# Holding the first five convolution taps of tile 0 behind the softmax's subtraction in even units

## The chip, the cores and the metric

The kernel runs on one core of one Trainium2 chip. The metric is device time in microseconds (us). Before the change the median of three runs is 3747.22 us (3746.66 to 3749.31). A core has five engines with their own instruction streams: TensorE (PE; its weight loads are listed as PEld), VectorE (DVE), ScalarE (ACT), GpSimd (POOL) and SyncE (SP), which issues the large DMAs. [...]

## The reference, cut to what matters

The input x is (8, 384, 64, 64) in f32: eight images of 384 channels. Two layers follow each other, each with a group norm in front and a residual addition behind.

```python
# layer 0: window attention, half of the heads on windows shifted by 4
x = x + attention(_gn(x))      # LayerNorm -> qkv -> two branches -> proj
#   per 8x8 window: softmax(q k^T * SCALE + bias [+ mask]) v
# layer 1: frequency filter on 8x8 blocks, depthwise 3x3 convolution, gate
x = x + ffn(_gn(x))
#   t = w_in . x ; t = irfft2(rfft2(t) * filter) ; t = conv3x3_depthwise(t)
#   x1, x2 = t[:, :192], t[:, 192:] ; out = w_out . (gelu(x1) * x2)
```

All of it is computed in f32, and the output is x after both layers.

## The kernel before

An image is cut into 8 strips of 8 rows (NS = 8); a strip is 384 channels by 512 pixels, held as 128 partitions by 3 tiles of 512. Time is counted in units. Unit u of an image covers one branch of one strip: even units the plain windows (br = 0), odd units the shifted ones (br = 1), so 16 units per image and 128 in all. While the attention of image b runs, the second layer of image b - 1 runs in the same units: a strip of it takes two units per stage, and its stages (mix, transform, back, convolution, gate, finish) follow each other over about six units.

The function calls are collected in a plan: at(place, piece, ...) gives each piece a place in units, and the pieces are called in the order of these places. On TensorE this order is kept, as every matmul and transpose is marked with keep_in_program_order. On the other engines the Tile scheduler orders the instructions: it keeps a simulated clock, and on each engine takes the earliest instruction of the program among those that it holds to be ready. An instruction planned late can so be taken early, in time that the engine would have stood idle. The function behind(i, other, NoSync, ...) adds an edge that keeps i after another instruction in this ordering, without a semaphore.

The pieces that matter here:

- scores (TensorE, PSUM tile pS), weights (VectorE: bias additions L456, maximum L460, subtraction L463, which is stored as zs["soft"]), exponent (ScalarE, L469), turn (TensorE transposes pT), apply (TensorE, pA) and normalise (VectorE: reciprocal L503 and product L504, the weighted values' norm), put (TensorE transposes po; copies L527 to L537). In the plan, weights of a unit stands at 0.12, and normalise of the unit before at 0.07.
- Projection: pr, with L546 adding the residual.
- LayerNorm: ln_sums (matmuls ln, ScalarE's m L347, VectorE's L349, L350 and L352, two DMAs that spread the line), ln_scale (VectorE, L363), shifted_half (GpSimd, L376 to L378).
- qk_tile (matmuls pq; ScalarE copies them to qab, kab, qcd, kcd, L394) and v_tile (pvv; L428).
- Second layer: mix (pt, copied by L584), transform (pf; product with the filter on VectorE, L601), back (pz, copied with borders by ScalarE, L629 to L633, to a tile z).
- conv: for each of the tiles m = 0, 2, 1 of a strip, the centre tap is a scaled copy by ScalarE (L667), and taps 1 to 8 are a chain of eight scalar_tensor_tensor on VectorE (L673), each adding a shifted z to the accumulator zz. Taps 1 to 5 use rows that are there once the strip's own z is; taps 6 to 8 need the first row of the next strip and come two units later. Taps 1 to 5 of tile 0 are planned at 0.68 to 0.92 of an even unit, those of tiles 2 and 1 in the odd unit after it, and taps 6 to 8 of the strip before at 0.20 to 0.45 of the even unit. All of b = B - 1, the last image, is left out of the rules below.
- gate (ScalarE's Gelu L686, L687; VectorE L688 to L690) and finish (matmuls pw; VectorE adds the residual from PSUM, L706; SyncE stores the strip). The maximum L460 of an even unit is held behind the last L706.

PSUM tiles of the pool "gemm" (four buffers) serve pq, pvv, pr, pt, pf, pz, pw and ln in turn; tiles of the pool "att" (two buffers) serve pS, pT, pA and po. TensorE waits for a buffer until it has been read.

The program also pads TensorE's stream with empty instructions. FETCHES counts instructions per piece, WAITS estimates the wait instructions (5.325 per unit), and RUN_AT gives the place within 256 at which a stretch is to begin; small_tiles marks where this is worked out.

Of the kernel before, what the change touches and what calls it, by code (L numbers as in the profile page):

```python
# [38 lines left out]
def block_kernel(ctx: ExitStack, tc: tile.TileContext, out, x, consts, fsel, wqk, wv, bqk, bv,  # L39
                 wp, bp, lng, lnb, rpb1, rpb2, w_in, w_dw, w_out, filt):  # L40
    nc = tc.nc
    B = x.shape[0]
# [35 lines left out]
    def row512(tag, bufs, name):  # L78
        return sb.tile([P, ST], F32, tag=tag, bufs=bufs, name=name)
# [209 lines left out]
    def behind(i, other, kind, reason):  # L289
        tc.add_manual_dep(i.ins, other.ins.name, mybir.DependencyInfo(kind, mybir.DependencyReason.DATA),  # L290
                          reason=reason)
# [366 lines left out]
    def conv(b, s, m, tap):  # L658

        z = zs[b, s, m]  # L660
        n = on_pe[s].get(m, 0) if b == B - 1 else 0
        if tap < max(n, 1):
            return
        if tap == max(n, 1):
            zz = row512("zz", 5, f"zz_{b}_{s}_{m}")
            if n == 0:
                nc.scalar.activation(zz.rearrange("p (r c) -> p r c", c=SW), z[:, 1:9, 1:SW + 1], AF.Copy,  # L667
                                     scale=dw_sb[:, m, 4:5])
                zs[b, s, "zz", m] = zz
            zs[b, s, "acc", m] = zz  # L670
        acc, old = zs[b, s, "acc", m], zs[b, s, "zz", m]
        dy, dx = TAPS[tap] // 3, TAPS[tap] % 3
        i = nc.vector.scalar_tensor_tensor(acc.rearrange("p (r c) -> p r c", c=SW),  # L673
                                           z[:, dy:dy + 8, dx:dx + SW], dw_sb[:, m, TAPS[tap]:TAPS[tap] + 1],
                                           old.rearrange("p (r c) -> p r c", c=SW), ALU.mult, ALU.add)

        if b < B - 1 and m and tap == 1:
            tc.keep_in_program_order(i)
        if b < B - 1 and tap == 6:
            behind(i, zs["soft"], mybir.DependencyClass.NoSync, "softmax first")  # L680
        zs[b, s, "zz", m] = acc

# [30 lines left out]
    for b in range(B):  # L713
# [62 lines left out]
        for s in range(NS):  # L776
            u = first + 2 + 2 * s
            at(u - 0.84, load, b, s, "mix")
            at(u + 0.02, normal_x1, b, s)
            for i in range(4):  # L780
                at(u + (0.28, 0.45, 0.60, 0.78)[i], mix, b, s, i)
            for j in range(2):
                at(u + (0.995, 1.02)[j], transform, b, s, j)
            if b < B - 1:
                at(u + 1.985, small_tiles, u + 2)
            at(u + 1.99, back, b, s)

            for n, m in enumerate((0, 2, 1)):
                for tap in range(1, 6):
                    at(u + (2.62, 3.15, 3.5)[n] + 0.06 * tap, conv, b, s, m, tap)  # L790
                for tap in range(6, 9):
                    at(u + 4.2 + 0.25 * (n * 3 + tap - 6) / 9, conv, b, s, m, tap)
            if b == B - 1:
                at(u + 2.3, conv_taps, b, s)
            at(u + 5.16, load, b, s, "finish")
            at(u + 4.5, gate, b, s)
            at(u + 6.10, finish, b, s)
# [130 lines left out]
```

## Time and profile before

| what | value |
|---|---|
| median of three runs | 3747.22 us |
| profiled execution, its own time | 3747.89 us |
| its span | 3745.9 us |
| TensorE busy, weight loads busy | 3638.7 us (97%), 2315.4 us (62%) |
| VectorE busy | 2838.6 us (76%) |
| ScalarE busy | 2378.3 us (63%) |
| GpSimd busy | 439.2 us (12%) |
| granted TensorE clock | 0.996 |
| L673, the taps on VectorE | 1490 instructions, 1105.9 us, mean 760 ns |

A line of a timeline has start, duration, engine, source line, operation, what it writes and reads, how many instructions were merged, and, in brackets, how long the engine stood idle before it and what ended that. Matmuls come from two helper functions, so nearly all of them carry L62 or L72 and are told apart by their tiles. In a list of waits a row tells who waited for whom, with us in total, times, and the longest in us.

### The profile page before, as it was taken

What the parts mean: (1) busy time and instruction counts of PE and PEld (TensorE: products, weight loads), DVE (VectorE), ACT (ScalarE), POOL (GpSimd) and SP (SyncE); (2) the same over time, 40 slices, a digit from 0 to 9 for tenths busy, and PEclk for the clock granted to TensorE, in tenths of its full rate; (3) what the DMA queues carried; (4) which work ended last, traced back from release to release, by engine and by line L of the source; (5) the groups of instructions that cost most, each with busy time, mean ns of one, the idle gap of its engine ahead of it and who ended that gap; (6) DMA issues with size and microseconds to landing.
All of it is one profiled execution on the core that took longest, in us unless ns stands there. A gap on an engine that the chain in (4) does not pass through costs nothing.

```text
span 3745.9 us, 92754 instructions
## 1 busy us (share of the span) xinstructions
PE 3638.7 (97%) x38144; PEld 2315.4 (62%) x38144; DVE 2838.6 (76%) x4601; ACT 2378.3 (63%) x3946; POOL 439.2 (12%) x776
## 2 busy tenths in 40 slices
PE   4999999999999999999999999999999999999898
PEld 3666666666666666666666666666666666666554
DVE  4554578777887687777887778877788777777898
ACT  1766676666676576665766766666676666676442
POOL 5111011111101011101101011111111111110000
PEclk9999999999999999999999999999999999999999
DMA  4222222323322233323332322323233222222422
GB/s 121 86 83 74 91 100 100 107 90 108 118 103 83 88 133 108 116 80 116 109 113 84 117 95 100 133 80 109 99 113 109 99 88 83 100 80 82 151 102 76
DMA packets 144506, 377.32 MB, mean 101 GB/s; under 512 B 12308, under 2 KB 12900, under 8 KB 144100
## 3 DMA queue, kind: packets, MB, share of 16 engines
q1 hardware_dynamic: 139952, 370.60, 28.3%
q8 instruction: 318, 5.21, 0.6%
q0 software_dynamic: 2048, 0.15, 0.1%
q10 hardware_dynamic: 2100, 0.63, 0.1%
q14 instruction: 88, 0.72, 0.1%
HBM read 270.54 MB, written 100.79 MB: 99 GB/s over the span
## 4 chain that ended last, share of the span: by engine, by line
PE 84%; DVE 6%; ACT 4%; DMA 3%; issue 2%; POOL 0%; SPq 0%; ACTq 0%; DVEq 0%; POOLq 0%
PE pq L62 23%; PE pr L62 13%; PE pt L62 12%; PE pvv L62 12%; PE pw L62 6%; PE pS L62 3%; PE pA L62 3%; PE pz L62 3%; DVE zz L673 3%; PE pT L72 3%; PE po L72 2%; PE pf L62 2%; PE ln L62 2%; PE pc L62 1%; DMA rpb_raw<-in_rpb_dram 1%
## 5 line engine op out<-in xcount | busy, mean ns | idle before, releaser
L673 DVE SCALAR_TENSOR_TENSOR zz<-z,dw_sb,zz 128x512 f32<-128x512 f32 x1490 | 1105.9, 760 | 195.4 <-ACT zz L667 172.7
L62 PE MATMUL pq<-y,wqk_sb 128*128 128x512 f32 x2160 | 990.2, 596 | 0.0
L62 PEld LDWEIGHTS pq<-y,wqk_sb 128*128 128x128 f32 x2160 | 402.7, 190 | 456.2 <-issue 424.2
L62 PE MATMUL pt<-wi_sb,xn 128*128 128x384 f32 x1536 | 535.2, 487 | 8.1 <-DVE x_finish L706 8.1
L62 PE MATMUL pr<-oT,wp_sb 128*128 128x512 f32 x1152 | 523.1, 592 | 1.0 <-DVE oT L537 1.0
L62 PE MATMUL pvv<-wv_sb,y 128*128 128x192 f32 x2880 | 496.5, 326 | 2.5 <-ACT kcd L394 2.5
L62 PEld LDWEIGHTS pvv<-wv_sb,y 128*128 128x128 f32 x2880 | 471.6, 190 | 40.1 <-issue 21.3
L394 ACT ACTIVATE qab<-pq,bq_sb,cst 96x512 f32<-96x512 f32 (+1 forms) x256 | 198.0, 773 | 402.9 <-PE pq L62 386.0
L62 PEld LDWEIGHTS pt<-wi_sb,xn 128*128 128x128 f32 x1536 | 286.0, 190 | 213.9 <-issue 49.0
L394 ACT ACTIVATE kcd<-pq,vec 32x512 f32<-32x512 f32 x512 | 348.9, 681 | 9.0
L62 PEld LDWEIGHTS pr<-oT,wp_sb 128*128 128x128 f32 x1152 | 211.1, 190 | 224.4 <-issue 209.7
L376 POOL COPY y<-y 128x384 f32<-128x384 f32 x112 | 100.2, 894 | 1583.1 <-PE pvv L62 1089.3
L349 DVE TENSOR_TENSOR lr<-m 128x128 f32<-128x128 f32 x64 | 19.7, 308 | 301.9 <-ACT m L347 301.8
L335 POOL TENSOR_TENSOR sq<-sq 128x512 f32<-128x512 f32 x128 | 167.8, 1311 | 637.2 <-ACT sq L333 632.2
L667 ACT ACTIVATE zz<-z,dw_sb 128x512 f32<-128x512 f32 x183 | 133.8, 733 | 166.1 <-PE pw L62 160.5
L394 ACT ACTIVATE qcd<-pq,bq_sb,cst 96x512 f32<-96x512 f32 (+1 forms) x256 | 197.3, 771 | 43.8 <-PE pq L62 40.4
L546 DVE SCALAR_TENSOR_TENSOR x_add<-pr,vec,x_add 128x512 f32<-128x512 f32 x192 | 143.4, 747 | 103.3 <-PE pr L62 101.5
L584 ACT COPY t<-pt 128x384 f32<-128x384 f32 x256 | 125.0, 488 | 141.6 <-PE pt L62 138.7
L428 ACT COPY v<-pvv 128x384 f32<-128x384 f32 x256 | 121.8, 481 | 129.7 <-PE pvv L62 129.3
L62 PE MATMUL pw<-zz,wo_sb 128*128 128x512 f32 x384 | 181.9, 610 | 0.0
L394 ACT ACTIVATE kab<-pq,vec 96x512 f32<-96x512 f32 (+1 forms) x256 | 174.4, 681 | 9.1 <-PE pq L62 7.4
L469 ACT ACTIVATE e<-e 128x1024 f32<-128x1024 f32 x128 | 135.3, 1057 | 68.2 <-DVE e L463 66.8
(139 smaller groups left out, 5272.6 us busy)
## 6 DMA issues: line engine op xcount, KB each, us to landing
x_add<-in_x_dram SPq DMA_DIRECT2D x64, 768.0 KB
x1d<-x_add SPq DMA_DIRECT2D x64, 768.0 KB
x_mix<-x1d SPq DMA_DIRECT2D x64, 768.0 KB
x_finish<-x1d SPq DMA_DIRECT2D x64, 768.0 KB
out_dram<-x_finish SPq DMA_DIRECT2D x64, 768.0 KB
x_norm<-in_x_dram SPq DMA_DIRECT2D x61, 768.0 KB
x_stats<-in_x_dram SPq DMA_DIRECT2D x56, 768.0 KB
rs<-line SPq DMA_DIRECT2D x62, 256.0 KB
```

The costliest lines, as they stand in the source:

```text
L62: tc.keep_in_program_order(nc.tensor.matmul(*args, **kw))
L72: tc.keep_in_program_order(nc.tensor.transpose(*args, **kw))
L335: nc.gpsimd.tensor_tensor(sq[:, 0, :], sq[:, 0, :], sq[:, k, :], ALU.add)
L349: nc.vector.tensor_tensor(rc, m[:, 0:P], m[:, 0:P], ALU.mult)
L376: nc.gpsimd.tensor_copy(dst[:, :, :, :, 0:4], src[:, :, :, :, 4:8])
L394: return nc.scalar.activation(dst[to:to + n], pq[of:of + n], AF.Identity, bias=bias[of:of + n], scale=scale)
L428: nc.scalar.copy(v[:, 2 * g:2 * g + 2, :, 0:HD], pvv[:, 0:384].rearrange("p (g h d) -> p g h d", g=2, h=4))
L469: nc.scalar.activation(e, e, AF.Exp)
L546: nc.vector.scalar_tensor_tensor(t[:, m, :], pr, bp_sb[:, m:m + 1], t[:, m, :], ALU.add, ALU.add)
L584: nc.scalar.copy(t1, pt[:, 0:C])
L667: nc.scalar.activation(zz.rearrange("p (r c) -> p r c", c=SW), z[:, 1:9, 1:SW + 1], AF.Copy, scale=dw_sb[:, m, 4:5])
L673: i = nc.vector.scalar_tensor_tensor(acc.rearrange("p (r c) -> p r c", c=SW), z[:, dy:dy + 8, dx:dx + SW], dw_sb[:, m, TAPS[tap]:TAPS[tap] ...
```

## The change

One condition is widened. Tap 6 of each tile was held behind the latest softmax subtraction already; now tap 1 of tile 0 is too, in all images but the last. As taps 2 to 5 add to the accumulator of tap 1, they follow it. At the place of this call in the plan the latest subtraction is that of the same even unit.

```diff
         if b < B - 1 and m and tap == 1:
             tc.keep_in_program_order(i)
-        if b < B - 1 and tap == 6:
+        if b < B - 1 and (tap == 6 or m == 0 and tap == 1):
             behind(i, zs["soft"], mybir.DependencyClass.NoSync, "softmax first")
         zs[b, s, "zz", m] = acc
```

## The prediction

> **What bounds the kernel now.** I read the page's busy times first, then the list of what TensorE waited for, then the timelines of two even units. The profiled execution took 3747.89 us with a span of 3745.9; 2.0 us lie around the span. The median of the runs is 3747.22, 0.7 below the profiled one.
>
> ```profile
> PE 3638.7 (97%) x38144; PEld 2315.4 (62%) x38144; DVE 2838.6 (76%) x4601; ACT 2378.3 (63%) x3946; POOL 439.2 (12%) x776
> ...
> q8 instruction: 318, 5.21, 0.6%
> ...
> PE 84%; DVE 6%; ACT 4%; DMA 3%; issue 2%; POOL 0%; SPq 0%; ACTq 0%; DVEq 0%; POOLq 0%
> ```
>
> TensorE (PE) is the bound, and its program order is fixed. Its busy time may hide pitch, so I also took the distance between successive matmul starts: from 600 to 3500 us it shows the same few stalls as the waits below and no others. VectorE (DVE, 76%) can only matter where TensorE waits for it, directly or through ScalarE (ACT). From the answer on TensorE's waits (us in total, times, longest):
>
> ```profile
> PE pT L72 <- ACT e L469: 9.0, 8, 1.4
> PE pz L62 <- DVE t L601: 8.9, 15, 3.0
> PE pt L62 <- DVE x_finish L706: 8.1, 6, 1.4
> PE pz L62 <- ACT v L428: 7.3, 13, 1.0
> ...
> PE pvv L62 <- ACT kcd L394: 2.5, 6, 0.6
> ```
>
> The third line is the one that VectorE's order in even units makes; the last is made through ScalarE. The first line's waits are nearly all in odd units, the second's in the last image, which the change leaves out. Now VectorE and TensorE around 1838 us, an even unit with the first strip of an image:
>
> ```profile
> 1828.70 0.26 DVE L503 RECIPROCAL rc<-pA 128x16 f32<-128x16 f32 x1
> 1828.99 0.96 DVE L504 TENSOR_TENSOR o<-pA,rc 128x768 f32<-128x768 f32 x1
> 1831.91 2.43 DVE L673 SCALAR_TENSOR_TENSOR zz<-z,dw_sb,zz 128x512 f32<-128x512 f32 x2 [1.96 <-ACT zz L667]
> 1834.26 0.68 DVE L456 TENSOR_TENSOR e<-pS,bias 128x512 f32<-128x512 f32 x1
> ...
> 1835.46 2.31 DVE L673 SCALAR_TENSOR_TENSOR zz<-z,dw_sb,zz 128x512 f32<-128x512 f32 x3
> 1837.69 1.88 DVE L706 TENSOR_TENSOR x_finish<-pw,x_finish 128x512 f32<-128x512 f32 x3
> ...
> 1840.72 1.22 DVE L463 TENSOR_TENSOR e<-e,mx 128x1024 f32<-128x1024 f32 x1
> ...
> 1838.42 2.20 PE L62 MATMUL pt<-wi_sb,xn 128*128 128x384 f32 x6 [1.35 <-DVE x_finish L706]
> ```
>
> Two and three taps (L673), five in all, stand ahead of the residual additions (L706) that empty the PSUM tiles pw; pt (the fence's last line, from TensorE's own timeline) needs a tile of the same pool and starts late. These five are taps 1 to 5 of tile 0. In the common even unit around 1210 us they begin even before the norm (L503, L504):
>
> ```profile
> 1210.26 1.54 DVE L673 SCALAR_TENSOR_TENSOR zz<-z,dw_sb,zz 128x512 f32<-128x512 f32 x2 [3.86 <-ACT zz L667]
> 1211.71 0.25 DVE L503 RECIPROCAL rc<-pA 128x16 f32<-128x16 f32 x1
> ...
> 1215.89 1.88 DVE L706 TENSOR_TENSOR x_finish<-pw,x_finish 128x512 f32<-128x512 f32 x3
> ...
> 1218.92 1.23 DVE L463 TENSOR_TENSOR e<-e,mx 128x1024 f32<-128x1024 f32 x1
> ```
>
> Here pt starts at 1218.73, 2.1 us after the first addition ended: no stall.
>
> **What the Trainium skill says.** "Perfetto Trace Analysis", Identifying the Most-Contended Engine: matmul busy time is a poor measure of distance to the limit, since matmuls overlap; I used start distances for that reason, and they agree with the waits. "SBUF — State Buffer", SBUF: two separate sides: a VectorE instruction with two SBUF inputs and a GpSimd one exclude each other on a shared port for a whole instruction. The trace agrees: the tap at 1832.70 took 1.64 us, against 0.74 usually, while GpSimd's addition of squares ran from 1830.83 to 1833.79. "Perfetto Trace Analysis", Identifying Dependency Chains: an instruction that waits for several engines may get EventSemaphore instructions ahead of it; TensorE shows 687. "Runtime: NRT & Kernel Launch", Instruction fetch mechanics: instructions are fetched in blocks of 256, mostly hidden; the 318 fetches of q8 are TensorE's 81,516 records divided by 256. The last two make my slower rival.
>
> **The change part by part.** It adds one ordering edge per tile 0, on one engine: no instruction, no DMA and, both ends being VectorE's, no semaphore wait. It concerns 54 even units (7 images by 8 strips, less two units after the last softmax). Five taps move behind the softmax's subtraction (L463). In front of them the nine last taps of the strip before are already held there and come earlier in the plan, so the five will mostly fill VectorE's gaps later in the unit.
>
> *First strips, six units with a stall* (942, 1390, 1838, 2286, 2735, 3184 us). By the rows above: the norm ends at 1829.95; the two bias additions take 1.27 (1834.26 to 1835.53) and end near 1831.2, pS being done at 1828.8; pw's last six matmuls start at 1830.78 with 0.43 us each, so the three tiles are ready near 1831.8, 1832.7 and 1833.5, and the first addition ends near 1832.5. The transposes po start at 1836.04, eight by 0.109 us, so pt can start at 1836.91 and has 4.4 us to spare. In these six units pt starts 1.62 us after the last po, in the other fifty 0.11: saved 6 x 1.51 = 9.1 us. (The waits row's 8.1 leaves out part of the pitch.)
>
> *Last strips of six images, and the very first unit*: matmuls pvv wait for ScalarE's kcd copies in six of them, the start distance after pT being 0.59, 0.61, 0.63, 0.68, 0.70 and 0.90 against 0.11 us: 3.5 us. Around 1780 the subtraction ends at 1791.27 with four taps in front of it, 4 x 0.73 = 2.9 us plus waits for the shared port. Without them: norm to 1780.6, statistics (1.87) to 1782.4, biases to 1783.5, additions to 1785.4, maximum and subtraction (1.20 + 1.21) to 1787.8. ScalarE's exponent, at 1791.30, is then held only by ScalarE itself, whose table load ended at 1789.47: 1.8 us earlier, and kcd was 0.5 to 0.8 us late. I take all 3.5; the bounds are 0 and 3.5.
>
> *The other 42 units*: no wait of TensorE here goes back to these taps. The exponent ends 5.2 us or more before its transposes in every even unit of the steady part. 0 us. What hides the moved 5 x 0.70 = 3.5 us (a row of five takes 3.51) is VectorE's idle time before the LayerNorm's first step (L349), 2.9 to 7.6 us in these units, plus about 1.1 us ahead of the gate. Around 1210: the norm no longer stands behind taps that wait for ScalarE and can start 1.5 us earlier, at 1210.2, but pw holds the additions until about 1216, so the subtraction gains about 1.6 of the 3.5 us and 1.9 are left to absorb, 0.8 after the gate's gap. That fits even 2.9. If that cover were gone, each us late at L349 passes through the LayerNorm's line DMAs to the odd unit's scaling (L363), subtraction and exponent; there the cover is 2.7 to 4.3 us, but only 0.05 to 0.4 us in one or two odd units per image.
>
> *Queues.* SyncE's store of the finished strip waits for the last addition, so it and the loads queued behind it leave 1.6 to about 3.4 us earlier; nothing waits longer. GpSimd's 2.6 to 3.0 us of squares run early in the first-strip units, where the taps leave; in the common unit GpSimd is almost idle until 1236.
>
> *Sum*: 9.1 + 3.5 = 12.6 against the profiled 3747.9, that is 3735.3; 3734.6 against the median. I predict 3735, whose own range is 3730 to 3740.
>
> **Rivals.** *No change that counts* (3740 to 3754). The planner places instructions by its own estimates. If it fills the place before the additions with other ready work (statistics, normalisation), or if a new wait of about 1 us per image appears on ScalarE, the 12.6 shrinks below 7.5. For it: nine of the 12 us sit in six units only. Against it: in those units VectorE stood idle for 1.96 us ahead of the taps, so nothing else was ready.
>
> *Slower through the instruction blocks* (3755 to 3785). The planner pads TensorE's stream so that block boundaries miss the stretch of tiny matmuls, with a fixed estimate of 5.325 wait instructions per unit. Counting TensorE's records, that stretch begins at place 241 of a block around 570 us and at 233 to 235 near the end. In the two early units where the place was 209 or 210, matmuls there started about 0.8 us late. If the new order takes away one wait instruction per two units, the place drifts some 50 by the end; it becomes slower once over half of the 50 even boundaries fall near 210 (30 x 0.8 = 24 us, less 12.6: 3759), and at worst 50 x 0.8 - 12.6 = +27, 3775. For it: the place is already at the lower edge, where single units show 0.3 to 0.4 us. Against it: waits per odd and even unit are the same (4; 5 to 8) whether taps stand before or behind the norm, apart from first strips, whose ScalarE order differs as well; and the other sign costs nothing (places 6 to 12 show no stall).
>
> *The edge does nothing*: excluded nearly, as the taps stand ahead of L463 in all these units.
>
> **How the numbers follow.** A measurement of this kernel tells about 0.2%, 7.5 us. The forecast has 0.55; no change 0.21; slower 0.24, most of it by the blocks, the rest by late LayerNorm lines or a ScalarE order that delays an evacuation. Faster by over 0.2% also holds if only the 9.1 come (3738), so faster 0.55, same 0.21, slower 0.24. The 8-in-10 range starts at 3730 and runs through the no-change case to 3760, where the slower case begins.
>
> **What would show it.** Right: the waits' row of pt for x_finish is gone; the row of pvv for kcd shrinks; no tap between L504 and L463 in even units; the idle time before L349 falls by 2 to 4 us and stays above zero. Wrong: new rows of pS, pA or pf with "issue", or pT waiting longer for e in odd units, or a new wait for ScalarE's copies.

## The result and the profile after

The median went from 3746.42 us (3745.36 to 3749.31, six runs) to 3731.30 us (3729.22 to 3733.45, six runs), 15.1 us less. The ratio is 0.996 with a 95% interval of 0.995 to 0.997; that is faster by more than the 0.2% that a measurement of this kernel can tell. The profiled execution took 3731.68 us with a span of 3729.9, 16.0 less than before at the same granted clock (0.995, was 0.996).

From the page after, busy times, the shares of the chain that ended last, and two groups of instructions (busy us, mean ns of one, and the engine's idle time before them with its releaser):

```profile
PE 3633.8 (97%) x38144; PEld 2313.8 (62%) x38144; DVE 2844.2 (76%) x4601; ACT 2383.2 (64%) x3946; POOL 435.5 (12%) x776
...
PE 88%; DVE 4%; ACT 3%; DMA 2%; issue 2%; POOL 0%; ACTq 0%; DVEq 0%; POOLq 0%; SPq 0%
...
L673 DVE SCALAR_TENSOR_TENSOR zz<-z,dw_sb,zz 128x512 f32<-128x512 f32 x1490 | 1081.8, 751 | 23.7 <-ACT z L632 11.2
```

Every count of instructions is the same. TensorE's share of the chain rose from 84 to 88%, VectorE's fell from 6 to 4%. The idle time before the taps fell from 195.4 to 23.7 us, nearly all of it on ScalarE's centre tap (L667) before. It did not vanish: in the list of VectorE's waits the idle time ahead of the norm rose from 29.0 to 151.3 us (L503) and that ahead of the additions from 5.0 to 77.8 us (L706).

TensorE's waits after (us in total, times, longest):

```profile
PE pT L72 <- ACT e L469: 9.4, 8, 1.5
PE pz L62 <- DVE t L601: 9.3, 15, 2.8
PE pz L62 <- ACT v L428: 6.6, 13, 1.0
```

The rows of pt for x_finish (8.1 us) and of pvv for kcd (2.5 us) are gone, the other three moved by at most 0.7 us. Measured by the distance from one matmul's start to the next, summed over the span by pairs of tiles, po to pt fell by 9.09 us and pT to pvv by 3.45.

VectorE in the first-strip unit that the prediction showed at 1838 us, now at 1822:

```profile
1822.47 0.96 DVE L504 TENSOR_TENSOR o<-pA,rc 128x768 f32<-128x768 f32 x1
1823.34 0.68 DVE L456 TENSOR_TENSOR e<-pS,bias 128x512 f32<-128x512 f32 x1
1823.94 0.68 DVE L456 TENSOR_TENSOR e<-pS,bias_odd 128x512 f32<-128x512 f32 x1
1825.41 0.69 DVE L706 TENSOR_TENSOR x_finish<-pw,x_finish 128x512 f32<-128x512 f32 x1 [0.79 <-PE pw L62]
...
1827.13 0.69 DVE L706 TENSOR_TENSOR x_finish<-pw,x_finish 128x512 f32<-128x512 f32 x1 [0.17 <-PE pw L62]
1827.74 1.21 DVE L460 TENSOR_REDUCE mx<-e 128x16 f32<-128x1024 f32 x1
1828.98 1.23 DVE L463 TENSOR_TENSOR e<-e,mx 128x1024 f32<-128x1024 f32 x1
1830.12 0.74 DVE L673 SCALAR_TENSOR_TENSOR zz<-z,dw_sb,zz 128x512 f32<-128x512 f32 x1
```

No tap stands between L504 and L463. The additions now wait for TensorE's pw, not TensorE for them: the first ends at 1826.10, and TensorE's timeline has pt 4.3 us later, directly behind the transposes:

```profile
1829.50 1.04 PE L72 MATMUL po<-cst,o 128*128 128x128 f32 x8
1830.38 2.10 PE L62 MATMUL pt<-wi_sb,xn 128*128 128x384 f32 x6
```

The chain behind kcd shows on ScalarE around a last strip. Before, at 1791 us:

```profile
1788.19 1.28 ACT L469 ACT_TABLE_LOAD   x1
1791.30 1.06 ACT L469 ACTIVATE e<-e 128x1024 f32<-128x1024 f32 x1 [1.83 <-DVE e L463]
```

and after, at 1783 us:

```profile
1781.98 1.28 ACT L469 ACT_TABLE_LOAD   x1
1783.27 1.06 ACT L469 ACTIVATE e<-e 128x1024 f32<-128x1024 f32 x1
```

The 1.83 us of waiting for the subtraction are gone; the exponent runs straight behind its table load.

### The profile page after: what moved, and what is told of

Read it like the earlier page. It is cut to its first block, busy times and chain, and to the rows that moved or that the text cites. A ratio compares the mean times of both kernels' runs of the same rounds, so it can differ in the third digit from the quotient of the medians.

```text
span 3729.9 us, 92790 instructions
## 1 busy us (share of the span) xinstructions
PE 3633.8 (97%) x38144; PEld 2313.8 (62%) x38144; DVE 2844.2 (76%) x4601; ACT 2383.2 (64%) x3946; POOL 435.5 (12%) x776
## 4 chain that ended last, share of the span: by engine, by line
PE 88%; DVE 4%; ACT 3%; DMA 2%; issue 2%; POOL 0%; ACTq 0%; DVEq 0%; POOLq 0%; SPq 0%
PE pq L62 24%; PE pr L62 13%; PE pt L62 13%; PE pvv L62 12%; PE pw L62 7%; PE pz L62 3%; PE pS L62 3%; PE pA L62 3%; PE pT L72 3%; PE po L72 3%; PE pf L62 2%; PE ln L62 2%; DVE zz L673 2%; DMA rs<-line 1%; PE pc L62 1%
## 5 line engine op out<-in xcount | busy, mean ns | idle before, releaser
L673 DVE SCALAR_TENSOR_TENSOR zz<-z,dw_sb,zz 128x512 f32<-128x512 f32 x1490 | 1081.8, 751 | 23.7 <-ACT z L632 11.2
L667 ACT ACTIVATE zz<-z,dw_sb 128x512 f32<-128x512 f32 x183 | 133.9, 733 | 171.5 <-PE pw L62 157.2
L335 POOL TENSOR_TENSOR sq<-sq 128x512 f32<-128x512 f32 x128 | 164.1, 1282 | 637.7 <-ACT sq L333 632.8
L349 DVE TENSOR_TENSOR lr<-m 128x128 f32<-128x128 f32 x64 | 19.7, 308 | 276.8 <-ACT m L347 276.7
L706 DVE TENSOR_TENSOR x_finish<-pw,x_finish 128x512 f32<-128x512 f32 x192 | 129.9, 689 | 77.8 <-PE pw L62 77.8
```

Of the source, the lines that this page charges most:

```text
L335: nc.gpsimd.tensor_tensor(sq[:, 0, :], sq[:, 0, :], sq[:, k, :], ALU.add)
L349: nc.vector.tensor_tensor(rc, m[:, 0:P], m[:, 0:P], ALU.mult)
L706: zs["added"] = nc.vector.tensor_tensor(t[:, m, :], pw[m], t[:, m, :], ALU.add)
```

## The experiments

My theory was that of the prediction: six first strips give 9.1 us and the last strips 3.5, because VectorE's additions and subtraction come free earlier; the other units give nothing. The rivals: the gain is spread over all units; it needs the place behind the subtraction; or TensorE's instruction blocks move it up or down. Three runs split the edge by strips, one moves its far end, two move the blocks, one breaks the cover, and one goes after the wait that is left.

**First strips alone.**

```diff
-        if b < B - 1 and (tap == 6 or m == 0 and tap == 1):
+        if b < B - 1 and (tap == 6 or m == 0 and tap == 1 and s == 0 and b):
```

> The edge stands only for strip 0 of images 1 and on (six even units with a stall of pt in the trace of before). Forecast's theory: TensorE waited for the residual additions that stood behind these five taps; 6 x 1.51 us of late start of pt, and some 0.1 us more per unit inside pt, come back: 9 to 10 us faster than before, the waits' row of pt for x_finish is gone, the row of pvv for kcd stays at about 2.5 us. Rival A, that the earlier subtraction and exponent of all even units make the gain: six of 54 units bring about a ninth of 15 us, 1.7 us. Rival B, that fewer collisions of taps with GpSimd on the shared port make it: the same ninth, though it would be the larger part, as squares run in these units.

Measured: 3736.80 us, 9.1 below the kernel before beside it (3745.93); ratio 0.9977 (0.9967 to 0.9986). TensorE's waits:

```profile
PE pvv L62 <- ACT kcd L394: 3.0, 7, 0.6
...
PE pt L62 <- DVE x_finish L706: 0.4, 1, 0.4
```

The start distances from po to pt fell by 8.21 us, the wait for kcd stayed. So the first strips give 8 to 9 us, where a gain spread over all even units would have brought 1.7.

**Last strips and the very first unit alone.** Edit: the condition ends `and (s == NS - 1 or s == b == 0)`.

> The edge stands only for strip 7, and for strip 0 of image 0. Forecast's theory: in these units the subtraction is late, with it exponent and Gelu on ScalarE, with these the kcd copies that pvv waits for; 3.5 us of late starts come back, and up to 1 us more inside pvv: 3 to 5 us faster than before; the row of pt for x_finish stays at 8.1 us, that of pvv for kcd is gone. Rival A: an eighth of 15 us, 2 us, with no row changed.

Measured: 3740.29 us, 5.6 below before and so a little more than the 3 to 5 expected; ratio 0.9986 (0.9979 to 0.9992). Now it is the other row that stays, and that of pvv for kcd is not in the list:

```profile
PE pt L62 <- DVE x_finish L706: 8.1, 6, 1.4
```

The distance pT to pvv fell by 3.45 us, as in the full change. The next distance, within pvv, fell by 0.69 more; the prediction did not count it, the expectation of this run did. Together that is 4.1 us.

**The middle strips alone.** Edit: the condition ends `and 0 < s < NS - 1`.

> The edge stands only for strips 1 to 6. Forecast's theory: no wait of TensorE goes back to the taps there, so the time is that of before within 2 us, with both rows (pt for x_finish 8.1 us, pvv for kcd 2.5 us) still there, though the subtraction is 1 to 2 us earlier in 41 units. Rival A: some 11 us faster (41 of 54 units).

Measured: 3745.15 us, 0.8 below before; ratio 1.0001 (0.9993 to 1.001). The taps of 41 units changed place, as their row on the page shows, while TensorE's two waits stayed:

```profile
L673 DVE SCALAR_TENSOR_TENSOR zz<-z,dw_sb,zz 128x512 f32<-128x512 f32 x1490 | 1094.1, 758 | 40.4 <-ACT zz L667 16.9
```

155 of the 195 us of idle time ahead of the taps went without a gain. That VectorE idles less in front of a line was worth nothing by itself here; four fifths of what the page seems to show as waste cost no time. The three ratios miss 1 by 2.3, 1.4 and -0.1 thousandths, 3.6 in all, against 4 (3 to 5) for the whole change.

**The far end of the edge at the additions.** The taps of tile 0 only have to follow the last L706, not the subtraction.

```diff
+        if b < B - 1 and m == 0 and tap == 1 and "emptied" in zs:
+            behind(i, zs["emptied"], mybir.DependencyClass.NoSync, "additions first")
...
+            zs["emptied"] = zs["added"]
```

> In place of the subtraction the last residual addition (L706) is what tap 1 of tile 0 is held behind; one or two taps then stand between the additions and the subtraction, and nothing is ahead of the additions. Forecast's theory: pt is freed as in the changed kernel (9 to 10 us); in the last strips the subtraction is about 0.75 us later than in the changed kernel and still 2.5 us earlier than before, and kcd had 0.5 to 0.8 us to make up, so the kcd gain stays too, but for image 0's first unit, which has no additions: 12 to 15 us faster than before. A rival by which the place behind the subtraction itself matters (the softmax's maximum and subtraction being back to back): half the gain or less.

Measured: 3732.72 us, 13.2 below before; ratio 0.9967 (0.9954 to 0.9979), not told apart from the full change. po to pt fell by 9.1 us, pT to pvv by 3.0, and one wait of 0.3 us for kcd is left. A tap now stands between subtraction and maximum, which delays the exponent by one tap. So what matters is that the additions and, in the last strips, most of the taps no longer stand in front; the place behind the subtraction is sufficient but not needed.

**The instruction blocks, twice.** The slower rival wanted the block boundary moved to near 210 at the end of the even units. The first attempt changed the first value, `RUN_AT = 183, 138`.

> The changed kernel with RUN_AT 183 in place of 208 for the stretch of tiny matmuls at the end of even units: 25 empty instructions fewer once, so that this stretch starts at places 216 to 208 of a block of 256 in place of 241 to 233. It prices the forecast's slower rival. If that rival's price holds (0.8 us per boundary near 210): 50 boundaries cost 30 to 45 us against the changed kernel, which gives 3755 to 3775, with pS or pA waiting for issue in nearly every even unit. If the place is not what cost 0.8 us in the two early units: 3731 within 3 us.

This missed its aim. Counted in TensorE's records, it moved the other stretch, that of pz, pA and pS at the end of odd units (pA's first matmul from places near 140 down to 120 to 112), and left that of the even units where it was. It measured 3736.99 us against 3748.91 for the kernel before on that chip; ratio 0.9967 (0.9953 to 0.998). It says nothing on the rival. The second attempt changed the other value, `RUN_AT = 208, 113`.

> The change with the second value of RUN_AT lowered by 25, from 138 to 113: the stretch of tiny matmuls at the end of the even units, which begins at place 241 to 233 of a block of 256 instructions, should begin at 216 to 208, where the slower rival of the prediction wants it; in two or three units of an image the padding would go over its limit and is left out, so that single stretches lie elsewhere. e5_place had moved the other stretch. The rival's price (0.8 us at each of up to 50 boundaries) gives 3731 + 25 to 40 = 3756 to 3771 us, with rows of pf, pA or pS with 'issue' in the list of TensorE's waits. If the place is worth nothing once it lies off the middle of a stretch, 3728 to 3735 us and no such rows.

Measured: 3735.04 us against 3746.85; ratio 0.9969 (0.9957 to 0.998). The even units' stretch now begins at 216 to 209 in 34 units. Beyond its shortest length in the trace (3.18 us from the start of the first pf to that of the last pS) the stretch lost 0.10 us per unit there, and as much in the 47 such units of the full change, which begin at 241 to 233. At 0.1 us, 50 boundaries cost 5 us, not the 40 us that the rival needed.

Where the padding went over its limit and was left out, in twelve odd units, the stretch of pA and pS fell to places 37 to 43 and 206 to 212. There it lost 0.6 to 1.3 us each beyond its shortest length (1.92 us from the first pA to the last pS), 9.7 in all. The list of TensorE's waits has it under "issue":

```profile
PE pS L62 <- issue: 7.7, 16, 1.1
```

Five waits and 2.5 us stood there in the full change. So the price of 0.8 us is real, but it belongs to a badly placed stretch of the odd units, whose start the padding otherwise puts at 145 to 137; the rival had it from two units at the very start, and a third one there, at 317 us and place 209, shows no stall. The Trainium skill ("Runtime: NRT & Kernel Launch", Instruction fetch mechanics) calls the crossing of a block boundary mostly hidden. The 34 even boundaries agree, the twelve odd ones do not.

**Taps ahead of the odd unit's norm.** To learn what lies beyond the cover, the five taps were kept from filling the gaps of the even unit: they follow the LayerNorm's reciprocal (L352), which ends near the next unit.

```diff
-        nc.vector.reciprocal(rc, rc)
+        zs["line"] = nc.vector.reciprocal(rc, rc)
...
-            behind(i, zs["soft"], mybir.DependencyClass.NoSync, "softmax first")
+            behind(i, zs["line" if tap == 1 else "soft"], mybir.DependencyClass.NoSync, "softmax first")
...
-                    at(u + (2.62, 3.15, 3.5)[n] + 0.06 * tap, conv, b, s, m, tap)
+                    at(u + (2.94, 3.15, 3.5)[n] + 0.06 * tap, conv, b, s, m, tap)
```

> Tap 1 of tile 0 is planned 0.32 of a unit later and held behind the LayerNorm's reciprocal (L352) at the end of the even unit, so that the five taps leave VectorE's idle time of the even unit and stand between the norm, the biases and the subtraction of the odd unit. It takes the cover away that the forecast named for the moved 3.5 us. Theory: four taps, 2.9 us, come ahead of the odd unit's subtraction, less the 1.9 us that the scaling (L363) and its wait took there; the exponent is about 1 us later, which the common odd units cover (2.7 to 4.3 us) and the one or two tight ones per image do not: 7 to 13 us slower than the changed kernel for that, and more if the norm's product comes too late for po or an addition L546 too late for pr: 3738 to 3770. If VectorE has room everywhere: 3731 within 3 us.

Measured: 3778.00 us; ratio 1.0078 (1.0064 to 1.0091), some 29 us above before and more than expected. TensorE's waits, two of them new:

```profile
PE po L72 <- DVE o L504: 15.1, 42, 0.7
PE pT L72 <- ACT e L469: 12.5, 8, 1.6
...
PE pw L62 <- ACT z L632: 4.5, 12, 0.7
```

Against the full change, start distances rose by 24.6 us from pq to po, 16.5 within pw and 4.5 from pq to pT. The first is direct: taps stand between and ahead of the reciprocal and the product of the odd unit's norm, and po waits. VectorE around 627 us:

```profile
626.86 0.25 DVE L503 RECIPROCAL rc<-pA 128x16 f32<-128x16 f32 x1
627.02 0.70 DVE L673 SCALAR_TENSOR_TENSOR zz<-z,dw_sb,zz 128x512 f32<-128x512 f32 x1
627.65 1.01 DVE L601 TENSOR_TENSOR t<-pf,feff 128x384 f32<-128x384 f32 x2
628.58 0.95 DVE L504 TENSOR_TENSOR o<-pA,rc 128x768 f32<-128x768 f32 x1
```

The second goes through ScalarE's order, in twelve units whose pw takes 1.1 to 1.7 us longer, 15.9 in all. In one of them VectorE's work of the odd unit ends late, its last normalisation (L328) at 1048.11 us; ScalarE's square (L333), which reads it, stands ahead of the copies of pz that make z. The last line is TensorE's:

```profile
1048.20 1.48 ACT L333 ACTIVATE sq<-y 128x1536 f32<-128x1536 f32 x1 [2.36 <-DVE y L328]
1049.60 0.64 ACT L629 ACTIVATE z<-pz 128x512 f32<-128x512 f32 x1
1050.12 0.19 ACT L632 COPY z<-pz 128x64 f32<-128x64 f32 x1
...
1050.37 1.93 PE L62 MATMUL pw<-g,wo_sb 64*64 64x512 f32 x10 [0.31 <-ACT z L632]
```

TensorE's last pz matmuls end at 1047.33, yet the first of their PSUM tiles, which pw takes next, is emptied only at 1050.31, 3.0 us behind them, and pw starts again right after that; in the same unit of the full change it is 1.4 us. That the square's place is what stretches pw rests on these lines and on the wait row above; it was not tried alone. The expectation had named a late product ahead of po without a price, and not the copies ahead of pw.

**The wait that is left.** In the waits after, pT for the exponent is first. It falls in the odd units of strip 1. There the transposes were moved behind the first v tile, and the exponent behind the copies of k (zs["keys"] is the last of those for the second of qk's three tiles; the line that sets it is left out).

```diff
-                at(w + 0.30, exponent, b, s, br)
-                at(w + 0.64, turn, b, s, br)
+                at(w + (0.37 if b and s == br == 1 else 0.30), exponent, b, s, br)
+                late = b > 0 and s == 1 and br == 1
+                at(w + (0.82 if late else 0.64), turn, b, s, br)
...
-        nc.scalar.activation(e, e, AF.Exp)
+        i = nc.scalar.activation(e, e, AF.Exp)
+        if b and s == br == 1:
+            behind(i, zs["keys"], mybir.DependencyClass.NoSync, "keys first")
```

> The changed kernel, and in the second odd unit of each image but the first (where TensorE has no projection to do and waits for the exponent): the transposes pT are planned at 0.82 in place of 0.64, behind the first v tile, and the exponent at 0.37 and behind the k copies on ScalarE. It aims at what the change left: pT's wait for e of 1.1 to 1.3 us in seven units, and pz's wait for a v copy of 0.3 us in six. Theory, that these waits are of order alone, as the one between pt and the additions was: 6 to 11 us faster than the changed kernel, 3720 to 3725. Rival, that ScalarE's chain behind the exponent is itself the bound there: the stall moves to pz or pA and the time stays at 3731 within 3 us.

Measured: 3725.71 us; ratio 0.9939 (0.9926 to 0.9951), 23.2 us below the kernel before on the same chip, against 15.1 for the full change. The two ratios' intervals just touch; the start distances, one profile each, fell as well: pq to pT -12.1, pvv to pT +7.6, pz to pz -5.5, pq to pvv +3.0 and pvv to pvv -1.1, that is -8.1. Its waits (its lines are numbered two to four higher):

```profile
PE pT L72 <- ACT e L471: 6.7, 8, 1.5
PE pz L62 <- ACT v L430: 4.5, 6, 0.8
```

All distances but that within pz add up to -2.7, which is the fall of the first row from 9.4 us to 6.7: pT is reached later, behind pvv, and waits less. The other 5.5 go with the second row, whose waits were 13 and are 6; the row itself fell by only 2.1 us, and that the earlier v copies bring the rest was not tried alone. This version is faster than the kernel before; that it is also faster than the full change is likely, but the two were not measured beside each other.

## Why the prediction was right, and where it was off

The forecast was 3735 us (3730 to 3740 for the likeliest case alone); the median is 3731.3. The direction, the mechanism and both terms of the sum stand; the sum was 12.6, the median fell by 15.1 and the profiled span by 16.0. Another 0.8 us of the distance from 3735 is the kernel before itself, whose median is 3747.22 over the three runs that the forecast had and 3746.42 over six.

*First strips.* 9.1 us forecast; po to pt fell by 9.09. That term left out the second step: once pt has started late, its next matmul starts late as well, and the distance within pt fell by another 0.67. Each of the six units is 1.60 to 1.63 us shorter, not 1.51.

*Last strips and the first unit.* 3.5 us forecast, all of it taken within bounds of 0 and 3.5; pT to pvv fell by 3.45. The choice of the upper bound rested on the table load that holds the exponent 1.8 us earlier, and the trace shows just that. Here too the step within pvv gives 0.69 more. So the mis-sized part of both terms is the neglect of the second step, 1.36 us together.

*What is left of the 16.0.* TensorE's start distances add up to 15.45 less. Beside the 13.9 above, the distance within pS fell by 1.78. It is below that of the kernel before in the profiles of all three split runs, by 1.4 to 2.7, the middle strips among them, which gained no time; so the profiled execution of before stood about 2 us high there. It sits in the stretches of tiny matmuls, at the block boundaries: what these stretches take beyond their shortest adds up to 11.3 us before, 9.2 after, and 7.2 to 9.5 in the split runs. The forecast, which saw no stalls between 600 and 3500 us beside those in its list of waits, had passed over these small ones. This and up to 1.0 us at the start of the program are scatter, not gain, as far as these runs tell.

*The other 42 units.* 0 us forecast, and the middle strips alone measured 1.0001. The cover held, but was sized loosely: the list at the end of the forecast wanted the idle time before L349 to fall by 2 to 4 us per unit. Its total fell from 301.8 to 276.7 us, 0.5 us for each of the 54 units; where it was 7.6 it is 5.8, where it was 2.9 it is 3.5. The forecast's own working for 1210 us, 0.8 us left after the gate's gap, was nearer than its list. In that unit the norm now ends at 1206.71, VectorE waits 1.23 us for pw, then the taps fill the gaps between the put copies:

```profile
1209.13 0.69 DVE L706 TENSOR_TENSOR x_finish<-pw,x_finish 128x512 f32<-128x512 f32 x1 [1.23 <-PE pw L62]
...
1213.84 0.74 DVE L673 SCALAR_TENSOR_TENSOR zz<-z,dw_sb,zz 128x512 f32<-128x512 f32 x1
1214.50 0.38 DVE L535 COPY oT<-po 64x224 f32<-64x224 f32 x1
1214.80 0.73 DVE L673 SCALAR_TENSOR_TENSOR zz<-z,dw_sb,zz 128x512 f32<-128x512 f32 x1
...
1233.41 0.29 DVE L349 TENSOR_TENSOR lr<-m 128x128 f32<-128x128 f32 x1 [5.80 <-ACT m L347]
```

*Queues.* "Nothing waits longer" held for TensorE only. VectorE's statistics (L237) wait 27.7 us for x_stats, 23.0 before, and SyncE's stores of x1d (L556) wait 193.7 us for ScalarE's qab, 108.2 before; neither shows in TensorE's waits. The finished strip's store leaves 1.6 us earlier against TensorE's schedule in the common unit (2.53 us ahead of pt, was 0.94). In the first strips it leaves 5.2 us earlier, more than the 3.4 forecast: the last addition ended 2.66 us behind the place where pt could have started (1839.57 and 1836.91 before) and ends 2.56 us ahead of it now (1827.82 and 1830.38). The 1.96 us of idle time ahead of the taps went with them.

*The rivals.* No change was wrong because the freed places were not filled: TensorE's waits show nothing new on ScalarE. Slower through the blocks was wrong in two of its steps. The wait instructions did not become fewer: 4 in odd units and 5 to 8 in even ones as before, and the stretch begins at 241 to 233 as before. And its price was taken from the wrong units, two of three early ones at places 209 and 210, as the last run on the blocks shows. The 0.24 given to slower was too much for a mechanism without a change in the count.

## What to carry to other kernels

Where one engine is the bound and its order is fixed, count only the places where its start distances grow, and ask for each what stands in front of its releaser on the other engine; 155 us of VectorE's idle time could move for nothing, while six waits of 1.5 us paid. To each such wait add the step behind it, which was worth another 0.1 us here. Work that is moved out of the way must land in a gap that is really free: the same five taps cost some 29 us when they came late in the unit, where they held up the norm and, through ScalarE's order, the emptying of PSUM.

## What was not expected of the hardware

The stalls at TensorE's block boundaries have one place. In all ten traces, wherever a matmul of pA or pS starts more than 0.12 us behind one of pz, pA or pS within these stretches (147 cases), it stands at place 193 or 194 of 256 in the count of TensorE's records. How much is lost there goes with how many tiny matmuls (pz, pf, pA, pS) of the same stretch ran before it: with fewer than 115 none of 211 stretches lost 0.1 us at this place, with 115 to 139 it was 124 of 977, and with 170 or more all 23, 0.5 to 1.3 us each. The twelve odd units of the last run on the blocks are of the third kind, its 34 even ones of the second. No run changed this number alone, so that it is the cause is not shown.

VectorE's busy time on the taps fell by 24.1 us with the same 1490 instructions (1105.9 to 1081.8); the split runs give 6.3, 6.3 and 11.8 of it. The durations alone add up to 14.2 us less (1132.9 to 1118.7); the other 9.9 are more overlap of taps that follow each other. All 85 taps that took over 900 ns before, and all 53 after, ran beside a GpSimd instruction; beside its addition of squares (L335) there were 33 of them before and 1 after, and the longest tap fell from 1648 to 1301 ns. Fewer such collisions did not make the gain: in the middle strips' run they fell to 14, and the time stayed.
